# Two attention layers in one kernel: layer 1's projections for the coming units in quarters, and the last unit's sums turned on the tensor engine

## The chip, the cores and the metric

The kernel runs on one core of one Trainium2 chip. A core has a tensor engine (PE in the profile, its weight loads PEld), a vector engine (DVE), a scalar engine (ACT), a gpsimd engine (POOL), and a sync engine (SP) which here only issues DMAs. Each engine works through its own instructions in order; they wait for one another by semaphores. The tensor engine writes to PSUM, eight banks of 128 x 512 fp32 values; everything else lies in SBUF or in HBM. The metric is the time of one execution on the device in microseconds.

## The reference

The input x is 2 x 256 x 64 x 64 in fp32: two images of 256 channels at 4096 places. Two layers follow one another. Layer 0 is a gated attention with four heads of 16 channels; it is not touched here. Layer 1 takes its result:

```python
qkv = jnp.einsum('oc,bchw->bohw', w_qkv, x) + b_qkv[None, :, None, None]
qkv = qkv.reshape(b, HEADS, 3 * head_dim, h * w)
q, k, v = jnp.split(qkv, 3, axis=2)
scale = 1.0 / jnp.sqrt(jnp.asarray(head_dim, x.dtype))
attn = jax.nn.softmax(jnp.einsum('bhdn,bhdm->bhnm', q, k) * scale, axis=-1)
out = jnp.einsum('bhnm,bhdm->bhnd', attn, v).reshape(b, c, h, w)
return jnp.einsum('oc,bchw->bohw', w_out, out) + b_out[None, :, None, None] + x
```

It has four heads of 64 channels, so each query is compared with 4096 keys. Everything is fp32.

## The kernel before

**Units and steps.** Layer 1's attention is cut into 32 units, numbered 0 to 31 here: an image b, a pair g of heads and a block j of 512 queries, j running fastest. The 4096 keys of a unit are 32 chunks of 128, and a step takes two of them, so a unit has 16 steps; US = 16 is that number. The loop at line 1206 goes over all steps t of all units. "Step r of a unit" means its r-th of these 16, from 0 to 15. A unit's scores are weighed and gathered LAG = 11 steps later, so each step holds the scores of one unit and the weighing of chunks 11 steps older. The 16 chunks of a half unit share one shift (their running maximum); a unit has NG = 2 such halves.

**A step.** `score` (line 848) makes the scores of each chunk: two matmuls, one for each head, into a pair of PSUM banks. `keep` takes their running maximum on the vector engine (line 876) and copies them to SBUF on the scalar engine (877), which frees the PSUM pair. `shift` (929) subtracts the shift of an older chunk on the vector engine, `weigh` (941) takes the exponential on the scalar engine and adds it to a sum on gpsimd (953), and `gather` (963) multiplies by the values. On the tensor engine a step is: both chunks' scores, then what hangs in the place "early", then the gather, then what hangs in "late". On the vector engine it is: first maximum, first shift, "early end", second maximum, "late end", second shift. On the scalar engine: exponential of the step before, first copy, first exponential, "early end", second copy.

**What hangs beside it.** `at(t, place, step)` hangs a function on a place of step t; `seq` keeps compute instructions in program order, while DMAs on SP are placed by the framework. All the small PSUM work shares one bank: `misc` (lines 651 and 777; the pool `psm` has one buffer), so each user waits until the one before it has been read. These are, by step r of a unit:

- 0 and 8: the running maximum of a half is transposed (`turn_max`, line 884) and reduced (`fold`, 901), in two parts, early and late; its row goes through HBM and back, and `place_shift` copies it to PSUM on the scalar engine two steps later (921).
- 1: the gathered sums of the unit before are transposed (`turn_sums`) and scaled to rows (`rows`, 1041), early and late.
- 2 and 3: `next_keys` computes the keys for the next eight units' block, one pass of 128 x 512 over 128 of the 256 channels a step, and `store_keys` copies them out on the scalar engine in step 3.
- 5 and 6: `next_values` computes the values, two of four blocks of 128 places a step (four matmuls of 128 x 128), and `store_values` copies them in step 6. Units 0 to 23 do this; keys and values go to HBM and come back when the eight units are done.
- 10 and 11: `next_queries` computes the next unit's queries, one pass a step, kept by `keep_queries` in step 11. Units 0 to 30 do this.
- 12: `total` sums the gpsimd sums over the partitions on the tensor engine (993), and `keep_total` copies the result (1001) and sends it through HBM (1006, 1008) to turn rows into columns; `add_sums` and `factors` make the scale factors of it.

**Output.** In units 18 to 21, image 0's finished attention is projected block by block (`project_out`, 1071, four matmul passes for each image half of 128 channels in two parts o, and `output`, 1079, which adds bias and x on the vector engine and stores after the second part). Even blocks do it in steps 4 and 7, odd ones in 13 and 15, all in the place "early".

**The end.** Image 1's output is projected after the last unit. `last_output` (line 1163) loads what of the attention is finished (1172) and three blocks of x (1176) on SP; `FILL` places the first half of the projection (1182, 1188) between the last steps; the last unit's rows are stored to HBM and read back as `last_att` (1058, 1064), and then the second half is projected (line 1238) and stored.

Of the kernel before, what the change touches and what calls it, by code (L numbers as in the profile page):

```python
# [8 lines left out]
F32 = mybir.dt.float32  # L9
AF = mybir.ActivationFunctionType  # L10
# [4 lines left out]
P = 128  # L15
NB = 512
C = 256
CC = C // P
H = 4
D0 = 16  # L20
D1 = 64
# [5 lines left out]
def conv_attention_kernel(  # L27
# [19 lines left out]
    nc = tc.nc  # L47
    B, _, N = x.shape
    NJ = N // NB
    NM = N // P  # L50
    PB = NB // P
# [3 lines left out]
    small = ctx.enter_context(tc.tile_pool(name="small", bufs=2))  # L55
# [70 lines left out]
    for s in range(3):  # L126
        t = const_prep.tile([P, CC, P], F32, tag=f"wpad{s}", name=f"wpad{s}")
# [11 lines left out]
    ident = const.tile([P, P], F32, tag="ident", name="ident")  # L139
# [72 lines left out]
    def at(t, place, step):  # L212
        extras.setdefault((t, place), []).append(step)
# [19 lines left out]
    with own0:  # L233
# [417 lines left out]
        def misc(name):  # L651
            return small_bank[0](name)
# [6 lines left out]
        def project_in(ps, xt, g, t, c):  # L659
            seq(nc.tensor.matmul(  # L660
                ps, w1[:, c, t, bass.ts(g, P)], xt[:, c, :], start=(c == 0), stop=(c == CC - 1)
            ))
# [21 lines left out]
        def keep_queries(u):  # L684
            b, g, j = u
            q, ps = qs1[u]
            seq(nc.scalar.activation(q, ps, AF.Identity, bias=b1[:, g, 0:1]))
            qs1[u] = q

        def values_in(ps, xt, g, k):  # L690

            for c in range(CC):
                seq(nc.tensor.matmul(
                    ps[:, bass.ts(k, P)], xt[:, c, bass.ts(k, P)], w1[:, c, 2, bass.ts(g, P)],
                    start=(c == 0), stop=(c == CC - 1),
                ))
# [71 lines left out]
    with (  # L768
# [33 lines left out]

        def next_keys(b, g, i, c):
            if c == 0:
                halves_of["k"] = misc(f"k1p_{b}_{g}_{i}")
            project_in(halves_of["k"], loaded["kv", b, g, i], g, 1, c)

        def store_keys(b, g, i):  # L810
            k = l1.tile([P, NB], F32, tag="kv", name=f"k1s_{b}_{g}_{i}")
            seq(nc.scalar.activation(
                k, halves_of.pop("k"), AF.Identity, bias=b1[:, g, 1:2]
            ))
            nc.sync.dma_start(out=kd[b, g, i], in_=k)

        def next_values(b, g, i, k):
            if k == 0:
                halves_of["v"] = misc(f"v1p_{b}_{g}_{i}")
            for n in (k, k + 1):  # L820
                values_in(halves_of["v"], loaded["kv", b, g, i], g, n)

        def store_values(b, g, i):
            loaded.pop(("kv", b, g, i))
            v = l1.tile([P, NB], F32, tag="kv", name=f"v1s_{b}_{g}_{i}")
            seq(nc.scalar.copy(v, halves_of.pop("v")))
            nc.sync.dma_start(out=vd[b, g, i], in_=v)

        def load_keys(b, g, i):
            k = l1o.tile([P, NB], F32, tag=f"k{i}", name=f"k1_{b}_{g}_{i}")  # L830
# [5 lines left out]
            nc.sync.dma_start(out=v.rearrange("p i h d -> p (i h d)"), in_=vd[b, g, i])  # L836
            vs[b, g, i] = v

        def next_queries(u, c):
            b, g, j = u  # L840
            if c == 0:
                q = l1x.tile([P, NB], F32, tag="q", name=f"q1_{b}_{g}_{j}")
                qs1[u] = q, misc(f"q1p_{b}_{g}_{j}")
            project_in(qs1[u][1], loaded["q", u], g, 0, c)
            if c == CC - 1:
                loaded.pop(("q", u))

        def score(t):
# [61 lines left out]
        def lose(u):  # L910

            b, g, j = u
            lost = small.tile([P, 2, PB], F32, tag="lost", name=f"lost_{b}_{g}_{j}")
            seq(nc.gpsimd.tensor_tensor(lost, negs.pop((u, 1)), negs.pop((u, 0)), ALU.subtract))
            losts[u] = lost
# [82 lines left out]
        def keep_total(u):  # L998
            b, g, j = u
            row = l1.tile([P, NB], F32, tag="kv", name=f"srow_{b}_{g}_{j}")  # L1000
            seq(nc.scalar.copy(
                row.rearrange("p (a m i) -> p a i m", m=P, i=2),
                srows[u].rearrange("p (a i m) -> p a i m", m=P, i=2),
            ))
            for m in range(2 * NG):
                nc.sync.dma_start(out=sum1[u][m : m + 1, :], in_=row[32 * m : 32 * m + 1, :])
            s = small.tile([P, NG, 2, PB], F32, tag="sums1", name=f"sums1_{b}_{g}_{j}")
            nc.sync.dma_start(
                out=s.rearrange("p n k (a i) -> p (n k a) i", i=2),
                in_=sum1[u].rearrange("m (a p i) -> p (m a) i", p=P, i=2),  # L1010
            )
            srows[u] = s
            seq(nc.scalar.activation(losts[u], losts[u], AF.Exp, scale=D1**-0.5))

        def turned(a, name):
            ps = misc(name)
            for i in range(PB):
                seq(nc.tensor.transpose(ps[:, bass.ts(i, P)], a[:, bass.ts(i, P)], ident))  # L1018
            return ps.rearrange("p (i k d) -> p k i d", k=2, d=D1)

        def add_sums(u):
            s, lost = srows[u], losts[u]
            seq(nc.gpsimd.tensor_tensor(s[:, 0], s[:, 0], lost, ALU.mult))
            seq(nc.gpsimd.tensor_tensor(s[:, 1], s[:, 1], s[:, 0], ALU.add))
# [52 lines left out]
        def output(b, j, o):  # L1077
            xt = loaded["xo", b, j]
            seq(nc.vector.scalar_tensor_tensor(
                xt[:, o, :], outs.pop((b, j, o)), bo1[:, o : o + 1], xt[:, o, :], ALU.add, ALU.add  # L1080
            ))
            if o == CC - 1:
                nc.sync.dma_start(
                    out=out[b, :, bass.ts(j, NB)].rearrange("(c p) n -> p c n", p=P), in_=xt
                )
# [12 lines left out]
        for n, u in enumerate(units):  # L1098
            b, g, j = u
            t0 = n * US  # L1100
            if n > 0:
                at(t0 - 9, "start", lambda u=u, b=b, j=j: fetch(("q", u), x1[b][j]))
                for c in range(CC):
                    at(t0 - 6 + c, "early", lambda u=u, c=c: next_queries(u, c))
                at(t0 - 5, "early end", lambda u=u: keep_queries(u))
            if n < len(units) - NJ:
                to = (*units[n + NJ][:2], j)
                at(max(t0 - 1, 0), "start", lambda to=to: fetch(("kv", *to), x1[to[0]][to[2]]))
                for c in range(CC):
                    at(t0 + 2 + c, "early", lambda to=to, c=c: next_keys(*to, c))  # L1110
                at(t0 + 3, "early end", lambda to=to: store_keys(*to))
                at(t0 + 5, "early", lambda to=to: next_values(*to, 0))
                at(t0 + 6, "early", lambda to=to: next_values(*to, 2))
                at(t0 + 6, "early end", lambda to=to: store_values(*to))

                t1 = (n // NJ * NJ + NJ - 1) * US
                at(t1 + 2 * j + 2, "start", lambda to=to: load_keys(*to))
                at(t1 + 2 * j + 3 + LAG, "start", lambda to=to: load_values(*to))
            for k in range(NG):
                t1 = t0 + (k + 1) * GS // 2  # L1120
                for i, place in enumerate(("early", "late")):
                    at(t1, place, lambda u=u, k=k, i=i: turn_max(u, k, i))
                    at(t1, f"{place} end", lambda u=u, k=k, i=i: fold(u, k, i))
                at(t1 + 2, "end", lambda u=u, k=k: place_shift(u, k))
            t1 = t0 + US + GS // 2
            at(t1 + 4, "early", lambda u=u: total(u))
            at(t1 + 4, "early end", lambda u=u: keep_total(u))
            at(t1 + 1, "late", lambda u=u: lose(u))
            at(t1 + 5, "late end", lambda u=u: add_sums(u))
            at(t1 + 7, "start", lambda u=u: factors(u))  # L1130
            for place, k in (("early", 1), ("late", 0)):
                at(t1 + 9, place, lambda u=u, k=k: turn_sums(u, k))
                at(t1 + 9, f"{place} end", lambda u=u, k=k: rows(u, k))
            if b < B - 1 and (g, j) == (PR - 1, NJ - 1):
                for i in range(NJ):
                    t1 = t0 + US + (i + 4) * GS // 2
                    at(t1, "start", lambda b=b, i=i: fetch_output(b, i))
                    for o, step in enumerate((t1 + 4 + i % 2, t1 + 7)):
                        at(
                            step, "early",  # L1140
                            lambda b=b, i=i, o=o: project_out(b, i, o, misc(f"o1_{b}_{i}_{o}")),
                        )
                        at(step, "early end", lambda b=b, i=i, o=o: output(b, i, o))

# [146 lines left out]
```

## Time and profile before

| | us |
|---|---|
| median of 3 runs | 4735.43 (4734.52 to 4735.52) |
| the profiled execution | 4733.19, span 4731.4 |
| busy: PE / DVE / ACT / POOL | 4486.2 / 3901.4 / 3428.9 / 2496.6 |
| one ordinary unit of layer 1, from one unit's sums to the next's | 80.4 |
| one without next keys and values (units 24 to 30) | 78.6 |
| those with output projections (18 to 21) | 83.7 to 91.9, as the sums of step 12 cut them |

The span begins with the program's first instruction and ends with its last; the small rest of the execution's time lies around it. Layer 0 takes the first 2080 us and is the same in both kernels. Matmuls are pipelined, so their busy time overstates their work a little, and one fp32 matmul leaves two records. A wait of an engine is put down to what ended it; in a step that is full on all engines, the time is set by the one that never waits, and a wait of that one is what costs. Where a length in us is named without a view, it is the difference of two starts in the timeline.

### The profile page before, as it was taken

How to read it: one execution, taken by the hardware profiler on the slowest of the kernel's cores; microseconds unless marked ns; L12 is line 12 of the kernel's file. 1: busy time of each engine (PE TensorE's matmuls, PEld its weight loads, DVE VectorE, ACT ScalarE, POOL GpSimd, SP SyncE). 2: the span in 40 equal slices, each digit the busy share in tenths (PEclk: the TensorE clock that was granted, in tenths of full speed). 3: DMA queues.
4: the chain of work that ended last, by engine and by line, in shares of the span. 5: the costliest groups of instructions: out<-in, count | busy, mean ns of one | idle time of the engine just before them, and what ended most of it. 6: DMA issues, size and time to landing. Idle time of an engine off the chain costs nothing. (4 is left out here: it accounts for less than half of the span.)

```text
span 4731.4 us, 70140 instructions
## 1 busy us (share of the span) xinstructions
PE 4486.2 (95%) x26998; PEld 1464.4 (31%) x26998; DVE 3901.4 (82%) x4520; ACT 3428.9 (72%) x4508; POOL 2496.6 (53%) x1294
## 2 busy tenths in 40 slices
PE   8999999999999999989999999999999999898997
PEld 3433333333333333332222322222232222222222
DVE  6777777777777777359999999999998899999996
ACT  3366666666666666668888888888887788888884
POOL 5300000000000000029999999999988889999994
PEclk9999999999999999999999999999999999999999
DMA  3100000000000000121111221112222222111113
GB/s 103 34 4 19 19 20 16 15 15 15 15 15 15 15 13 13 57 63 39 34 41 34 66 45 34 41 34 54 59 52 65 65 63 56 37 26 23 26 34 83
DMA packets 200211, 174.67 MB, mean 37 GB/s; under 512 B 122168, under 2 KB 123000, under 8 KB 199748
## 3 DMA queue, kind: packets, MB, share of 16 engines
q1 hardware_dynamic: 198068, 169.60, 14.2%
q8 instruction: 212, 3.47, 0.3%
q14 instruction: 123, 1.01, 0.1%
q10 hardware_dynamic: 1808, 0.59, 0.1%
HBM read 127.66 MB, written 42.48 MB: 36 GB/s over the span
## 5 line engine op out<-in xcount | busy, mean ns | idle before, releaser
L953 POOL TENSOR_TENSOR acc<-acc,raw 128x1024 f32<-128x1024 f32 x883 | 2095.1, 2373 | 106.0 <-ACT raw L941 52.0
L402 DVE TENSOR_REDUCE mx<-a 128x1 f32<-128x512 f32 x2048 | 1314.5, 685 | 451.1 <-PE a L398 449.9
L439 ACT ACTIVATE p<-s 128x512 f32<-128x512 f32 x2048 | 1108.0, 595 | 702.6 <-PE a L398 369.1
L859 PE MATMUL s<-q,k 64*128 64x512 f32 x4096 | 1127.3, 639 | 180.3 <-ACT raw L877 175.5
L929 DVE TENSOR_TENSOR raw<-raw,shift 128x1024 f32<-128x1024 f32 x1024 | 1233.7, 1208 | 10.6 <-ACT shift L921 10.1
L876 DVE TENSOR_TENSOR rmax<-s,rmax 128x1024 f32<-128x1024 f32 x960 | 1167.0, 1216 | 88.7 <-PE s L859 85.6
L436 PE MATMUL s<-q,kT 32*128 32x512 f32 x4096 | 1218.5, 640 | 0.0
L877 ACT COPY raw<-s 128x1024 f32<-128x1024 f32 x1024 | 1035.4, 1011 | 237.9 <-DVE rmax L876 170.4
L941 ACT ACTIVATE raw<-raw 128x1024 f32<-128x1024 f32 x1024 | 1086.1, 1061 | 137.9 <-DVE raw L929 102.1
L398 PE MATMUL a<-kT,q 32*128 32x512 f32 x4096 | 1130.0, 643 | 0.9 <-DVE mx L402 0.8
L963 PE MATMUL av<-raw,v 128*64 128x512 f32 x4096 | 999.1, 606 | 6.3 <-ACT raw L941 6.0
L451 PE MATMUL av<-p,v 128*32 128x256 f32 (+1 forms) x7904 | 650.1, 399 | 0.6 <-ACT avs L465 0.6
L859 PEld LDWEIGHTS s<-q,k 64*128 64x128 f32 x4096 | 317.3, 185 | 921.1 <-ACT raw L877 725.0
L501 POOL TENSOR_TENSOR f<-f,dyn 128x16 f32<-128x16 f32 x15 | 3.3, 221 | 1028.1 <-DVE f L500 1028.1
L436 PEld LDWEIGHTS s<-q,kT 32*128 32x128 f32 x4096 | 397.4, 183 | 426.2 <-issue 392.8
L963 PEld LDWEIGHTS av<-raw,v 128*64 128x64 f32 x4096 | 243.8, 136 | 618.4 <-issue 465.2
L451 PEld LDWEIGHTS av<-p,v 128*32 128x32 f32 x7904 | 157.6, 108 | 751.5 <-issue 737.3
L552 POOL TENSOR_SCALAR res<-res 128x1024 f32<-128x1024 f32 x16 | 16.7, 1045 | 661.9 <-ACT res L551 661.9
L398 PEld LDWEIGHTS a<-kT,q 32*128 32x128 f32 x4096 | 304.8, 183 | 31.6 <-DVE mx L402 18.5
L951 POOL TENSOR_TENSOR acc<-raw,raw 128x1024 f32<-128x1024 f32 x64 | 152.5, 2382 | 157.1 <-ACT raw L941 157.1
L901 DVE TENSOR_REDUCE negs<-rt 128x4 f32<-128x512 f32 x128 | 88.1, 689 | 51.0 <-PE rt L884 50.9
L306 DVE RECIPROCAL std<-std 128x128 f32<-128x128 f32 x64 | 56.1, 919 | 37.4 <-ACT std L301 37.4
(319 smaller groups left out, 1721.9 us busy)
## 6 DMA issues: line engine op xcount, KB each, us to landing
row<-neg SPq DMA_DIRECT2D x128, 256.0 KB
x<-in_x_dram SPq DMA_DIRECT2D x16, 512.0 KB
res<-in_x_dram SPq DMA_DIRECT2D x16, 512.0 KB
x<-res SPq DMA_DIRECT2D x16, 512.0 KB
att<-rows SPq DMA_DIRECT2D x63, 128.0 KB
kd<-k1s SPq DMA_DIRECT2D x24, 256.0 KB
vd<-v1s SPq DMA_DIRECT2D x24, 256.0 KB
k<-kd SPq DMA_DIRECT2D x24, 256.0 KB
```

The lines of the kernel that those rows point to most:

```text
L398: seq(nc.tensor.matmul(ps, qs0[u][r, bass.ts(i, P)], kTs[b][r, bass.ts(m, NB)], start=True, stop=True,))
L402: seq(nc.vector.tensor_reduce(mxs[u][:, i * H + h, m : m + 1], ps, AX.X, ALU.max))
L436: seq(nc.tensor.matmul(ps, kTs[b][r, bass.ts(m, P)], qs0[u][r, :], start=True, stop=True))
L439: seq(nc.scalar.activation(pt[:, k, :], ps, AF.Exp, scale=D0**-0.5))
L451: seq(nc.tensor.matmul(avs[u][32 * h : 32 * h + 32, cols], vs0[b][:, m, 32 * h : 32 * h + 32], pts[t, h // 2][:, h % 2, cols], start=(m == ...
L859: seq(nc.tensor.matmul(ps[:, k, :], ks[b, g, m // PB][r, bass.ts(m % PB, P)], qs1[u][r, :], start=True, stop=True,))
L876: seq(nc.vector.tensor_tensor(rmax[u, n], ps, before, ALU.max))
L877: seq(nc.scalar.copy(raw, ps))
L929: seq(nc.vector.tensor_tensor(raws[t], raws[t], shifts[u, t % NM // GS], ALU.add))
L941: seq(nc.scalar.activation(p, p, AF.Exp, scale=D1**-0.5))
L953: seq(nc.gpsimd.tensor_tensor(accs[u, n], accs[u, n], p, ALU.add))
L963: seq(nc.tensor.matmul(avs1[u, n][k * D1 : (k + 1) * D1, :], v[:, m % PB, k, :], raws[t][:, k, :], start=(m % GS == 0), stop=(m % GS == GS ...
```

## The change

**Quarters.** `quarter` computes half of the channels' pass for half of the columns: one matmul of 128 x 256, where `project_in` had one of 128 x 512. Keys take one quarter in each of steps 2, 3, 4 and 5 and are stored in step 5. Values take one block of 128 places in each of steps 6, 7, 9 and 10; each pair has its own use of the misc bank and its own half copy on the scalar engine, in steps 7 and 10. Queries take two quarters in step 11 and one each in 13 and 14, with half copies in 11 and 14; the misc bank is thus free for the sums in step 12.

**Output projections.** Even blocks go to steps 5 and 7, odd ones to 12 and 15; all but the last of these four lie in the place "late", behind the gather.

**The last unit's sums.** They are copied as they lie, transposed on the tensor engine (`turn_total`, four transposes into the misc bank) and copied by the vector engine into the form in which the others come from HBM. The five DMAs of the last unit's sums are gone.

```diff
-        def next_keys(b, g, i, c):
-            if c == 0:
+        def quarter(ps, xt, g, t, q):
+
+            c, cols = q % 2, bass.ts(q // 2, NB // 2)
+            seq(nc.tensor.matmul(
+                ps[:, cols], w1[:, c, t, bass.ts(g, P)], xt[:, c, cols],
+                start=(c == 0), stop=(c == CC - 1),
+            ))
+
+        def next_keys(b, g, i, q):
+            if q == 0:
                 halves_of["k"] = misc(f"k1p_{b}_{g}_{i}")
-            project_in(halves_of["k"], loaded["kv", b, g, i], g, 1, c)
+            quarter(halves_of["k"], loaded["kv", b, g, i], g, 1, q)
...
-        def next_values(b, g, i, k):
-            if k == 0:
-                halves_of["v"] = misc(f"v1p_{b}_{g}_{i}")
-            for n in (k, k + 1):
-                values_in(halves_of["v"], loaded["kv", b, g, i], g, n)
+        def next_values(b, g, i, q):
+            if q % 2 == 0:
+                halves_of["vp"] = misc(f"v1p_{b}_{g}_{i}_{q}")
+            values_in(halves_of["vp"], loaded["kv", b, g, i], g, q)
...
+        def store_values(b, g, i, half):
+            if half == 0:
+                halves_of["v"] = l1.tile([P, NB], F32, tag="kv", name=f"v1s_{b}_{g}_{i}")
+            v, cols = halves_of["v"], bass.ts(half, NB // 2)
+            seq(nc.scalar.copy(v[:, cols], halves_of.pop("vp")[:, cols]))
+            if half == 1:
+                loaded.pop(("kv", b, g, i))
+                nc.sync.dma_start(out=vd[b, g, i], in_=v)
...
+            if q % 2 == 0:
+                halves_of["q"] = misc(f"q1p_{b}_{g}_{j}_{q}")
+            quarter(halves_of["q"], loaded["q", u], g, 0, q)
+
+        def keep_next_queries(u, half):
+            cols = bass.ts(half, NB // 2)
+            seq(nc.scalar.activation(
+                qs1[u][:, cols], halves_of.pop("q")[:, cols], AF.Identity,
+                bias=b1[:, u[1], 0:1],
+            ))
+            if half == 1:
                 loaded.pop(("q", u))
...
             row = l1.tile([P, NB], F32, tag="kv", name=f"srow_{b}_{g}_{j}")
+            if u == units[-1]:
+                seq(nc.scalar.copy(row, srows[u]))
+                seq(nc.scalar.activation(losts[u], losts[u], AF.Exp, scale=D1**-0.5))
+                srows[u] = row
+                return
...
+        def turn_total(u):
+
+            ps = misc("sumt")
+            for i in range(PB):
+                seq(nc.tensor.transpose(ps[:, bass.ts(i, P)], srows[u][:, bass.ts(i, P)], ident))
+            s = small.tile([P, NG, 2, PB], F32, tag="sums1", name="sums1_last")
+            seq(nc.vector.tensor_copy(
+                s.rearrange("p n k i -> p i (n k)"),
+                ps.rearrange("p (i m e) -> p i m e", i=PB, e=32)[:, :, :, 0],
+            ))
+            srows[u] = s
...
-                for c in range(CC):
-                    at(t0 - 6 + c, "early", lambda u=u, c=c: next_queries(u, c))
-                at(t0 - 5, "early end", lambda u=u: keep_queries(u))
+                for q in range(4):
+                    at(t0 - (5, 5, 3, 2)[q], "early", lambda u=u, q=q: next_queries(u, q))
+                at(t0 - 5, "early end", lambda u=u: keep_next_queries(u, 0))
+                at(t0 - 2, "early end", lambda u=u: keep_next_queries(u, 1))
...
-                for c in range(CC):
-                    at(t0 + 2 + c, "early", lambda to=to, c=c: next_keys(*to, c))
-                at(t0 + 3, "early end", lambda to=to: store_keys(*to))
-                at(t0 + 5, "early", lambda to=to: next_values(*to, 0))
-                at(t0 + 6, "early", lambda to=to: next_values(*to, 2))
-                at(t0 + 6, "early end", lambda to=to: store_values(*to))
+                for q in range(4):
+                    at(t0 + 2 + q, "early", lambda to=to, q=q: next_keys(*to, q))
+                    at(t0 + (6, 7, 9, 10)[q], "early", lambda to=to, q=q: next_values(*to, q))
+                at(t0 + 5, "early end", lambda to=to: store_keys(*to))
+                for i, step in enumerate((t0 + 7, t0 + 10)):
+                    at(step, "early end", lambda to=to, i=i: store_values(*to, i))
...
+            if u == units[-1]:
+                at(t1 + 5, "early", lambda u=u: turn_total(u))
...
-                    for o, step in enumerate((t1 + 4 + i % 2, t1 + 7)):
+                    for o in range(CC):
+                        step = t1 + ((5, 7), (4, 7))[i % 2][o]
+                        place = "early" if i % 2 and o else "late"
                         at(
-                            step, "early",
+                            step, place,
                             lambda b=b, i=i, o=o: project_out(b, i, o, misc(f"o1_{b}_{i}_{o}")),
                         )
-                        at(step, "early end", lambda b=b, i=i, o=o: output(b, i, o))
+                        at(step, f"{place} end", lambda b=b, i=i, o=o: output(b, i, o))
```

More of the change, by code (lines that the diff above doesn't have):

```diff
@@ L815, in store_keys @@
             nc.sync.dma_start(out=kd[b, g, i], in_=k)
-        def next_values(b, g, i, k):
-            if k == 0:
-                halves_of["v"] = misc(f"v1p_{b}_{g}_{i}")
-            for n in (k, k + 1):
-                values_in(halves_of["v"], loaded["kv", b, g, i], g, n)
[L823 to L827, printed above, removed]
+        def next_values(b, g, i, q):
[10 more added lines that the diff above has]
+                nc.sync.dma_start(out=vd[b, g, i], in_=v)
         def load_keys(b, g, i):
@@ L837, in load_values, with next_queries @@
             vs[b, g, i] = v
-        def next_queries(u, c):
+        def next_queries(u, q):
             b, g, j = u
[L841 to L845, printed above, removed]
+            if q == 0:
+                qt = l1x.tile([P, NB], F32, tag="q", name=f"q1_{b}_{g}_{j}")
+                qs1[u] = qt
+            if q % 2 == 0:
[8 more added lines that the diff above has]
+            if half == 1:
                 loaded.pop(("q", u))
```

## The prediction

> **What bounds the kernel now.** I read the waits of the vector engine in layer 1 first, then the busy sums of single units, then the timeline of three kinds of step, and last the chain that ended last. In what follows "step r" is step r of a unit's 16; s0 and s1 are the two score pairs of a step on the tensor engine (L859), rmax0 and rmax1 their maxima on the vector engine (L876), copy0 and copy1 their copies on the scalar engine (L877).
>
> The waits of the vector engine from 2080 us on (total, times, longest):
>
> ```profile
> DVE rmax L876 <- PE s L859: 83.2, 166, 1.3
> DVE negs L901 <- PE rt L884: 50.9, 95, 2.8
> ```
>
> Three units by window, an ordinary one, one with output projections, one without next keys (window, length, then busy time of PE, PEld, DVE, ACT, POOL):
>
> ```profile
> 2428.80:2509.20 80.40, 75.03 (x314) 23.35 (x312) 75.83 (x71) 69.72 (x75) 74.27 (x36) 1.00 0.16 37
> 3557.50:3646.70 89.20, 82.89 (x330) 25.97 (x328) 78.87 (x75) 69.79 (x75) 74.18 (x36) 1.00 0.25 69
> 4299.00:4377.70 78.70, 71.29 (x294) 20.63 (x292) 75.63 (x71) 68.98 (x73) 74.31 (x37) 1.00 0.14 24
> ```
>
> The vector engine is busy 75.8 of 80.4 us and the tensor engine 75.0: the vector engine bounds a unit and loses 4.6 us in it, to late scores and to the turned maxima. A unit without keys and values is only 1.7 us shorter, though 3.7 us of tensor time are gone: most of that work is hidden already. So the pool that a better spread can win is small: 1.7 us in 23 units, and 0.7 in 30 for the queries (from one copy0 to the next, step 11 takes 4.87 us with them and 4.18 in the last unit, which computes none).
>
> A step that carries half the values, one with an output projection and a plain one, from the timelines of the tensor and of the vector engine (start, us):
>
> ```profile
> 3033.76 1.16 PE L693 MATMUL v1p<-w,xb_('kv', 1, 0, 4)_24784 128*128 128x128 f32 x8
> 3034.85 1.94 PE L963 MATMUL av<-raw,v 128*64 128x512 f32 x8
> 3036.72 1.13 PE L859 MATMUL s<-q,k 64*128 64x512 f32 x4
> ...
> 3617.00 1.98 PE L1071 MATMUL o<-ao_('ao', 0, 2)_28123,wo 128*128 128x512 f32 x4
> ...
> 4590.32 1.13 PE L859 MATMUL s<-q,k 64*128 64x512 f32 x4
> 4591.92 1.13 PE L859 MATMUL s<-q,k 64*128 64x512 f32 x4 [0.47 <-ACT raw L877]
> 4592.98 1.94 PE L963 MATMUL av<-raw,v 128*64 128x512 f32 x8
> 4594.85 1.13 PE L859 MATMUL s<-q,k 64*128 64x512 f32 x4
> ```
>
> ```profile
> 3037.89 1.23 DVE L876 TENSOR_TENSOR rmax<-s,rmax 128x1024 f32<-128x1024 f32 x1 [0.69 <-PE s L859]
> ...
> 3619.03 0.75 DVE L1079 SCALAR_TENSOR_TENSOR xo_('xo', 0, 2)_28121<-o,bo,xo_('xo', 0, 2)_28121 128x512 f32<-128x512 f32 x1 [0.74 <-PE o L1071]
> ...
> 4591.82 1.22 DVE L876 TENSOR_TENSOR rmax<-s,rmax 128x1024 f32<-128x1024 f32 x1
> ```
>
> They give the rules of the sum. A score pair can be read 1.17 us after its start (3036.72 to 3037.89). s0 follows s1 by 2.93 us plus the step's extra work X (4591.92 to 4594.85, where X is 0), or by 2.82 plus X where s1 came straight after s0, 0.97 behind it. rmax0 repeats every 4.52 us, rmax1 is 2.26 behind it, copy1 1.30 behind rmax1, and s1 of the next step 1.07 behind copy1. So s0 has 0.33 us to spare in a plain step (4590.32 + 1.17 against 4591.82); what exceeds it becomes idle time of the vector engine, and the 0.47 us for which s1 waits anyway keeps the lateness from piling up. An extra ahead of copy1 on the scalar engine has 0.23 to spare (the next instruction can follow an exponential by 0.96, copy1 starts 1.19 behind it).
>
> The end, from the chain of waits (start, us):
>
> ```profile
> 4686.52 9.00 DMA sum_(1, 1, 7)_19383<-srow
> ...
> 4702.19 2.58 DMA att<-rows
> ...
> 4704.91 5.50 DMA last_att<-att
> ```
>
> The last unit's sums cross HBM behind 3.25 MB of loads on SP's queue (L1172, L1176), and all that leads to the last projection (4710.51) waits for them.
>
> **What the Trainium skill says.** "PSUM — Partial Sum Buffer", PSUM bank collisions: two engines on one bank are kept apart by a dependency, reads included. The trace agrees: copy0 starts 0.08 us after rmax0 ends. The one "misc" bank thus serializes its users. "DMA: Bandwidth & Descriptors", queues, rings and completion order: SP's copies stand in one ring on each of the 16 DMA engines, taken in order; here four copies of 2 KB took 9.00 us. "TensorE: Matmul & The Clock Gate", what's actually happening: an idle window of about 3.4 us halves the clock. Here eight records of L1182 took 5.57 us at 4700.37, after 13.5 us of idling, and 3.70 at 4680.09.
>
> **Ordinary units (1 to 23).** The matmul work stays. A pass of 128x512 costs 1.06 us (3063.88 to 3064.94), half the values 1.09 (3033.76 to 3034.85), a block of 128 columns of them thus 0.545. Time goes with columns from the one to the other, so I take 0.53 for a quarter of 256. New X: 0.53 in steps 2 to 5, 0.545 in 6, 7, 9 and 10, 1.06 in 11 (two quarters), 0.53 in 13 and 14. I carry the rules on from rmax0 of step 2 of a unit without keys (4254.57).
> Steps 2 to 4: s0 has 0.90 us to spare in step 3, 0.21 in 4, 0.07 in 5; rmax0 of step 5 gets 0.47 late (0.61 before). In step 5 the key store (0.57 in a row) slips copy1 by 0.34, and s1 of step 6 with it; with the first block of values rmax0 of step 7 is 1.04 late. Step 7's block adds 0 to 0.1; its half store (0.3) all but fits. At step 8 the lateness is 1.1, where the traced units with and without keys differ by 1.74 (29.02 and 27.28 us from rmax0 of step 2): gain 0.63. The same rules give the starts of the unit before, as traced, within 0.1 us.
> Step 9 has 1.13 us of waiting on the tensor engine: free. Step 10 loses a query pass and gets a block: 0.23 late. In 11 a half keep (0.33) replaces a keep (0.57), but the scalar engine is back to back from 10 to 12: 0.31 is won by step 13, and 0.10 given back in 14. Gain 0.21.
> Sum: 0.84 x 23 = 19.3 us. Units 24 to 30 have queries alone: 0.28 x 7 = 2.0. On SP the loads of x now stand behind the moved stores, but each is fetched about a unit ahead of its use: nothing. Unit 0, whose steps have no gather: nothing.
>
> **Output projections (units 18 to 21).** Three of four move from the early place to the late one. Before, the four cost 1.84, 1.51, 1.29 and 1.52 us (their steps less those of ordinary units). Late, the 1.92 us of matmuls stand behind the gather; the vector engine has done rmax1 by then and idles until they end, and the last shift and rmax0 of the next step are queued behind L1079. In step 5 they also wait until the key store frees the bank. By the rules the pair of steps 5 and 7 costs 5.5 against 3.35 (3.4 in step 5, part of it in place of lateness that is there anyway), step 12, behind the sums' matmuls, 2.66 against 1.29; step 15 stays. Loss 3.6 x 4 = 14.4 us. The store of an even block goes out 1.1 us nearer to the maxima of step 8; their row is issued by 3631.5 and used at 3637.19 without a wait: nothing.
>
> **The end.** Four transposes (0.6), a small vector copy (0.2, as the reciprocal of 8 columns), then the old steps: rows of half 1 start at 4686.3 instead of 4698.71. Late next is L1188 of the sixth block, ahead of half 0's rows on the vector engine: its load ends at about 4690.3 (3.25 MB move from 4680.0 to 4694.5). The att store goes out at 4693.2, not 4702.2, lands behind the last load, is read back from 4696.6 for 5.5 us, and the projection starts at 4702.1, not 4710.5: 8.4 us. The half clock may take 0 to 2 of it: 7.5. Bounds 4 and 10.
>
> **Sum.** 19.3 + 2.0 - 14.4 + 7.5 = 14.4 us off the profiled execution's 4733.2 (span 4731.4): 4718.8. The runs' median is 2.2 above it: 4721.
>
> **Rivals.** (a) The quarters hide entirely: 1.7 x 23 + 0.7 x 30 = 60 us, 7.5 at the end, less 14: 4682. For it: 0.47 us of tensor waiting in a plain step is nearly a quarter. Against: s0 has only 0.33, and the scalar engine its backlog. (b) Gain and loss cancel: projections cost 5 us more a unit, the ordinary gain is 0.5: 13 - 20 + 7 = 0, 4735. (c) Slower: a group of matmuls has a cost of its own beyond its columns. A unit gets 11 groups of such work instead of 6. The value records show none, but no quarter of 256 columns is in the trace; bounds 0 and 0.4 us. From 0.2 us on it decides: at 0.3 the 5 more cost 1.5, the gain of 0.84 turns into a loss of 0.66 x 23 = 15, and 15 + 14 - 7 = 22 us: 4757. (d) The turn at the end gains 3 us, as the store queues behind loads: 4725, inside the forecast.
>
> **How the numbers follow.** Forecast (with d) 0.60, (a) or half of it 0.10, (b) 0.19, (c) 0.11. An error of 0.3 us in a unit's gain is 8 us, of 1 us in the projections 4, at the end 3: its own range is 4709 to 4732. For 8 in 10 with the others: 4701 to 4744. The measurement tells about 0.2%, 9.5 us: faster 0.66, same 0.22, slower 0.12.
>
> **What would show it.** Units of 79.5 us instead of 80.4, of 78.4 instead of 78.7 where only queries are left, 90 to 95 in units 18 to 21, where L1079 waits longer for PE; waits of rmax for PE in small pieces over steps 5 to 7; no sums in the last chain, and the last projection 23 us after the last gather instead of 31. Wrong it would be if a quarter costs over 0.2 us in a plain step, if late projections cost nothing, or if a row of maxima comes late in step 10.

## The result and the profile after

| | before | after |
|---|---|---|
| median of 20 runs each, us | 4737.51 (4734.52 to 4740.97) | 4730.76 (4725.74 to 4734.27) |
| the profiled execution (span), us | 4733.19 (4731.4) | 4731.40 (4729.6) |

The change takes 6.75 us off; the ratio is 0.9985, with a 95% interval of 0.9978 to 0.9992. The two profiled executions lie only 1.8 us apart, because that of before is 4.3 us below its kernel's median and that of after 0.6 above. So the parts below are read in units and steps, which repeat within 0.05 us but for single late rows of maxima (rows that come back from HBM after their step wants them), and summed against the medians.

The waits of the vector engine in layer 1 of after (total, times, longest), and ahead of them the one of before that the prediction does not show:

```profile
DVE raw L929 <- ACT shift L921: 10.1, 6, 3.1
DVE rmax L895 <- PE s L878: 59.2, 130, 1.6
DVE negs L920 <- PE rt L903: 49.1, 91, 1.5
DVE raw L948 <- ACT shift L940: 17.6, 15, 3.7
```

The scores are late by 59 us in all instead of 83, in 130 places instead of 166. That is what quarters were to do. But 24 us less waiting did not make 24 us: added up over all of image 0's blocks, the waits for projections (L1079 before, L1115 after) rose from 15.6 to 33.2 us, and those for late shifts from 10.1 to 17.6. Of these 7.5 us only 2.5 lie in units 19 to 22; the others are single late rows. The profiled execution of before had few of those, which fits its lying so far below its median.

Three units by window, ordinary (12), with projections (20) and without next keys (27), here from copy0 to copy0, first before, then after; columns as in the prediction, which shows other units, cut at the sums:

```profile
3007.60:3087.90 80.30, 74.93 (x314) 23.35 (x312) 75.74 (x71) 69.73 (x74) 74.20 (x37) 1.00 0.17 37
3665.40:3757.30 91.90, 85.99 (x330) 26.88 (x328) 78.93 (x75) 69.72 (x74) 74.18 (x36) 0.96 0.25 66
4243.90:4322.50 78.60, 71.19 (x294) 20.64 (x292) 75.52 (x71) 68.88 (x73) 74.25 (x37) 1.00 0.12 24
```

```profile
2999.20:3079.00 79.80, 75.68 (x322) 24.76 (x320) 75.97 (x71) 69.50 (x76) 74.23 (x37) 1.00 0.17 37
3661.60:3757.30 95.70, 86.14 (x338) 28.53 (x336) 78.62 (x75) 69.73 (x76) 74.10 (x36) 0.96 0.24 63
4248.00:4326.50 78.50, 71.64 (x298) 21.24 (x296) 75.66 (x71) 68.75 (x73) 74.17 (x37) 1.00 0.14 25
```

The ordinary unit is shorter by 0.5 us and unit 27 by 0.1, at nearly the same busy time of the vector engine. Unit 20 has grown from 91.9 to 95.7.

Step by step, from the start of copy0 to that of the next step (us; units 18 to 22 stand beside unit 12, which has no projection):

| step of unit 12 | 2 | 3 | 4 | 5 | 6 | 7 | 11 | 13 | 14 | whole unit |
|---|---|---|---|---|---|---|---|---|---|---|
| before | 5.34 | 4.75 | 4.23 | 5.31 | 4.87 | 4.52 | 4.87 | 4.52 | 4.59 | 80.35 |
| after | 5.33 | 4.18 | 4.78 | 4.53 | 5.19 | 4.53 | 4.53 | 4.56 | 4.82 | 79.83 |

| what a projection adds to its step, unit 18 less unit 12 | first | second | first, odd block | second, odd block | given back or added next to them | sum |
|---|---|---|---|---|---|---|
| before (steps 4, 7, 13, 15) | 1.85 | 1.51 | 1.29 | 1.52 | 0 | 6.2 |
| after (5, 7, 12, 15) | 3.35 | 3.04 | 2.64 | 1.39 | -0.67 in 6, -0.36 in 8 | 9.4 |

Step 5 of unit 20 in after, first the tensor engine's timeline, then the vector engine's (start, us, and in brackets the idle time ahead with its releaser):

```profile
3693.70 1.94 PE L982 MATMUL av<-raw,v 128*64 128x512 f32 x8
3696.40 1.98 PE L1107 MATMUL o<-ao_('ao', 0, 4)_28774,wo 128*128 128x512 f32 x4 [0.76 <-ACT k1s L820]
```

```profile
3694.60 1.22 DVE L895 TENSOR_TENSOR rmax<-s,rmax 128x1024 f32<-128x1024 f32 x1
3698.42 0.75 DVE L1115 SCALAR_TENSOR_TENSOR xo_('xo', 0, 4)_28772<-o,bo,xo_('xo', 0, 4)_28772 128x512 f32<-128x512 f32 x1 [2.61 <-PE o L1107]
```

The projection waits 0.76 us for the bank behind the key store, although the gather ahead of it is done, and the vector engine, which has nothing else in its order, idles 2.61 us until it ends.

The chain that ended last, first two pieces of before, then after:

```profile
4678.88 0.44 PE late_sums L973 x2
...
4710.51 15.68 PE o L1182 x32
```

```profile
4683.40 0.44 PE late_sums L992 x2
...
4684.78 12.03 DMA x_last<-x
...
4697.59 0.74 DVE x_last L1229
4698.34 0.61 DVE rows L1077
4698.99 0.04 issue
4699.04 0.70 DVE rows L1088
4699.76 2.56 DMA att<-rows
...
4702.47 5.69 DMA last_att<-att
4708.16 0.09 issue
4708.25 16.36 PE o L1223 x32
```

The last unit's sums cross HBM no more. What is late next is the x block of L1229, as predicted. From the end of the sums' matmuls to the projection it is 24.4 us (4708.25 - 4683.84) instead of 31.2 (4710.51 minus 4679.32, the end of L973), and the projection itself takes 16.36 instead of 15.68: 6.1 us in all.

### The profile page after: what moved, and what is told of

It is laid out like the page before. It is cut to its first block, busy times and chain, and to the rows that moved or that the text cites. A ratio compares the mean times of both kernels' runs of the same rounds, so it can differ in the third digit from the quotient of the medians.

```text
span 4729.6 us, 70682 instructions
## 1 busy us (share of the span) xinstructions
PE 4509.2 (95%) x27222; PEld 1503.3 (32%) x27222; DVE 3905.8 (83%) x4521; ACT 3423.9 (72%) x4563; POOL 2496.6 (53%) x1294
## 3 DMA queue, kind: packets, MB, share of 16 engines
q1 hardware_dynamic: 197020, 169.58, 14.4%
## 5 line engine op out<-in xcount | busy, mean ns | idle before, releaser
L948 DVE TENSOR_TENSOR raw<-raw,shift 128x1024 f32<-128x1024 f32 x1024 | 1236.1, 1211 | 19.0 <-ACT shift L940 17.6
```

The source lines that it names most:

```text
L948: seq(nc.vector.tensor_tensor(raws[t], raws[t], shifts[u, t % NM // GS], ALU.add))
```

## The experiments

E1 to E3 take the change apart; E4 moves the work that had become dear; E5 to E8 test reasons one by one; E9 and E10 measure the disputed price. Ratios are against before, with 95% intervals. E1 to E4, E5 to E8, and E9 with E10 ran in three groups on three chips, each with runs of before beside it: 4738.31, 4736.87 and 4738.61 us. A difference between kernels of two groups is uncertain by these 2 us as well.

**E1: the turned sums alone.** Before, with `turn_total`, its call and the branch of `keep_total` that copies the last sums as they lie; nothing else.

> The kernel before with the last unit's sums turned on the tensor engine, and nothing else of the change. Theory (the three parts add up; the end is worth what the trace of after shows, 31.2 us from the end of the last gather to the last projection before and 24.4 after, less 0.7 for the half clock): 6 us less than before, about 4731.5. Rival (the end gives only 3 us alone, and the whole change's 6.75 us stem from its loops): about 4734.5.

Measured 4731.08, before beside it 4738.31: ratio 0.9985 (0.9978 to 0.9991), 7.2 us less. The end carries its part alone, and it is as large as what the whole change brings. So the loops' gains and losses must nearly cancel, within the 3 us of the interval.

**E2 and E3: both kernels without the projections.**

```diff
-            if b < B - 1 and (g, j) == (PR - 1, NJ - 1):
-                for i in range(NJ):
...
```

> The kernel before without the output projections of image 0 and their loads and stores: it leaves that output out. Units 18 to 21 took 86.5, 89.2, 91.9 and 88.2 us against 80.4. Theory (all of this excess is the projections'): 34 us less than before, about 4703. Rival (part of the excess is traffic or late rows of maxima that stay): 25 us less or fewer.

> The changed kernel without the output projections of image 0: it leaves that output out. Theory (late projections cost 14 us more than early ones; quarters gain 4 in unit 0 and some 0.5 a unit after it, 14 in all; the end 6): 49 us less than after, about 4682, and 20 us less than the kernel before without them. Rival (the projections cost the same in both places and the quarters gain next to nothing): 34 us less than after, 4697, and some 7 us less than the kernel before without them.

Measured 4700.56, ratio 0.9918 (0.9905 to 0.9932), and 4679.38, ratio 0.9875 (0.9860 to 0.9891). The projections thus cost 37.8 us early (4738.31 - 4700.56) and 51.4 late (4730.76 - 4679.38): the move loses 13.6. Without them the change gains 21.2, of which 7.2 is the end if it is worth the same here: the quarters are worth 14.0. That 14.0 - 13.6 + 7.2 comes near 6.75 proves nothing, since all three are differences of the same medians and have to add up to the change.

A test is the sum of the steps, which does not use the medians. Ordinary units give 23 x 0.52 us, units with queries alone 7 x 0.06 and unit 0 about 0.5 (see below): 12.9 for the quarters. Projections lose 4 x 3.2 = 12.8, and the end gains 6.1. 12.9 - 12.8 + 6.1 = 6.2, against 6.75. Late rows, which differ from one execution to the next, are left out of it.

**E4: the projections moved to units 24 to 31.** These compute no keys and values, so the misc bank and the tensor engine have room where the others have none.

```diff
...
-                    t1 = t0 + US + (i + 4) * GS // 2
-                    at(t1, "start", lambda b=b, i=i: fetch_output(b, i))
...
+                    t1 = END - (NJ - i) * US
+                    at(t1 - 2, "start", lambda b=b, i=i: fetch_output(b, i))
+                    for o, steps in enumerate(((2, 3, 4, 5), (6, 7, 9, 10))):
+                        for q, step in enumerate(steps):
+                            at(t1 + step, "early",
+                               lambda b=b, i=i, o=o, q=q: project_out(b, i, o, q))
...
-            at(END - 12 + 2 * i, "start", lambda i=i: fetch_last(i))
+            at(END - 12 + 2 * i + (i >= 3), "start", lambda i=i: fetch_last(i))
```

> The changed kernel with image 0's output projections in units 24 to 31, which compute no keys and values: one block a unit, in quarters of 256 columns in the steps and places of the keys and values (2 to 5, 6 and 7, 9 and 10, early), bias and sum on the vector engine in steps 5, 7 and 10. Theory (a quarter hides where the step has room, and the vector engine's 0.75 + 2 x 0.42 us are all that a unit pays, with 0.3 us of lateness): 49 us go in units 18 to 21, 8 x 1.9 = 15 come, about 4697. Rival (the loads of output blocks and the stores delay the rows of maxima or the last loads of x, or a projection costs 3.6 us wherever it is): no gain on after, 4720 to 4735.

Measured 4700.77, ratio 0.9921 (0.9907 to 0.9934): 37.5 us faster than before and 30 faster than after. The edit changes three things at once, the units, the cut of each projection into quarters and the place, and no run parts them. The window of a unit that now holds a block, and of an ordinary one:

```profile
4204.10:4285.00 80.90, 75.87 (x314) 23.81 (x312) 77.37 (x74) 68.85 (x73) 74.23 (x37) 1.00 0.19 43
2991.00:3070.90 79.90, 75.71 (x321) 24.80 (x321) 76.01 (x71) 69.57 (x76) 74.25 (x37) 1.00 0.18 37
```

A block costs 2.4 us (unit 27: 80.93 from copy0 to copy0, against 78.55 in after). In after, two blocks cost 9.6 to 15.9 us in each of units 18 to 21 (89.39 to 95.77 against 79.83). Of the 2.4, 1.7 is vector work (77.37 against 75.66), which nothing hides. The late rows of maxima of units 19 to 22 are gone too: in layer 1 up to 4720 us the waits for shifts are

```profile
DVE raw L948 <- ACT shift L940: 7.6, 17, 1.2
```

instead of 17.6 us, the longest 1.2 instead of 3.7.

**E5: the output loads two steps later.** `at(t1, "start", ...)` of `fetch_output` becomes `at(t1 + 2, "start", ...)`.

> The changed kernel with the loads of a block of output (x and attention, 512 KB each) two steps later, in steps 2 and 10 instead of 0 and 8, so behind the rows of maxima on SP's queue. Theory (at step 0 the load of x waits for the store of the block before, issued 4.5 us earlier, and keeps SP from the row of maxima behind it; its shift comes late in step 2, which takes 7.3 to 9.0 us in units 19 to 22 against 5.3 elsewhere): steps 2 to 4 of these units fall to 5.3, 4.2 and 4.8, and 12 us go, about 4719. Rival (the late row is due to other traffic, or the loads now come late for the projections of steps 4 and 5): no more than 3 us, 4728 or over.

Measured 4729.88, ratio 0.9986 (0.9979 to 0.9992): no gain on after. The timelines of SP's queue tell why, after first, then E5:

```profile
3658.32 0.38 SPq L1119 DMA_DIRECT2D out_dram<-xo_('xo', 0, 3)_28520  x1
3662.87 0.36 SPq L656 DMA_DIRECT2D xo_('xo', 0, 4)_28772<-x  x1
3663.28 0.46 SPq L923 DMA_DIRECT2D neg<-negs  x1
```

```profile
3659.05 0.38 SPq L1119 DMA_DIRECT2D out_dram<-xo_('xo', 0, 3)_28588  x1
3663.68 0.36 SPq L656 DMA_DIRECT2D xo_('xo', 0, 4)_28852<-x  x1
3664.09 0.46 SPq L923 DMA_DIRECT2D neg<-negs  x1
```

The order is the same: store, load of x, and then the row of maxima (L923). The framework places DMAs on SP by itself, and the later call did not move the load behind the row. So neither theory was tested. That the row suffers from the block's load and store ahead of it remains an argument; E2 and E3, without them, show only that the wait needs these projections or their traffic (7.7 us in E3).

**E6 and E7: keys and values alone, queries alone.** The quarters of each on before without projections.

> The kernel before without image 0's output projections, with the keys and values in the new quarters and the queries as before: it leaves image 0's output out. Against the same without the quarters (4700.6). Theory (the keys and values carry the gain, 0.46 us a unit by the steps of the traces, and 1.4 in unit 0): 12 us less, 4688.5. Rival (the gain is as much the queries'): 7 us less, 4693.5.

> The kernel before without image 0's output projections, with the queries in the new quarters and the keys and values as before: it leaves image 0's output out. Against the same without the quarters (4700.6). Theory (step 11 gains 0.34 us and steps 13 and 14 give 0.26 back): 0.07 us a unit, 2 us less, 4698.5. Rival (as predicted, 0.21 to 0.28 a unit): 7 us less, 4693.5.

E6 took 4762.79 us, ratio 1.0055 (1.0042 to 1.0067), 62 us more than E2, against both expectations. Steps 2 to 9 of its unit 12 are those of after, but step 10 takes 7.86 us and not 5.33. There the last block of values and the old first pass of the queries meet in the misc bank; the tensor engine, then the vector engine:

```profile
3087.03 0.71 PE L693 MATMUL v1p<-w,xb_('kv', 1, 0, 4)_24832 128*128 128x128 f32 x4
3089.61 1.12 PE L660 MATMUL q1p<-b_('q', (0, 1, 5))_25062,w 128*128 128x512 f32 x2 [1.87 <-ACT v1s L834]
3090.67 1.94 PE L973 MATMUL av<-raw,v 128*64 128x512 f32 x8
```

```profile
3093.71 1.23 DVE L886 TENSOR_TENSOR rmax<-s,rmax 128x1024 f32<-128x1024 f32 x1 [3.24 <-PE s L869]
```

The query pass waits 1.87 us for the half copy of the values, the gather waits behind the pass, and the next scores behind the gather. E6 says nothing of the keys' gain, but it shows what the queries' move is for: two users of the one bank in one early place cost 2.5 us in step 10, and 2.7 in the unit (82.49 against 79.83).

E7 took 4696.49, ratio 0.9914 (0.9901 to 0.9928), 4.1 less than E2, between the two expectations; with each set against before in its own group, it is 2.6 less. Step 11 takes 4.53 instead of 4.87, step 14 4.84 instead of 4.59; a unit is 0.05 us shorter (unit 12 80.32 and not 80.36; unit 27 78.56, and 78.61 in before). The steps thus give under 2 us, and the rest is within what the two groups differ by and what single late rows (step 2 of units 3, 16 and 22 in E2) make of a run. With the queries at 2 to 4, the keys and values get 10 to 12 of the 14.0.

**E8: the place late, in the old steps.** Before, with `"late"` for all but the last of the four projections.

> The kernel before with the output projections in its own steps (4 and 7, 13 and 15), but all except the last of these four in the place late, as the change has it. Theory (the place alone makes them dear: the matmuls stand behind the gather and the vector engine waits for their end): 3 us a unit more than early, 12 us in all, about 4750. Rival (late costs no more than early, and it is the new steps 5 and 12, where the key store or the sums stand ahead of it): 0 to 3 us more, 4738 to 4741.

Measured 4741.68, ratio 1.0011 (1.0002 to 1.0019), 4.8 more than before: nearer to the rival. Steps 4, 7 and 13 cost 2.56, 1.89 and 2.0 us instead of 1.85, 1.51 and 1.29, and 0.7 comes back in steps 5, 6 and 8: 7.3 us a unit instead of 6.2. Step 4 of its unit 20:

```profile
3694.14 1.94 PE L963 MATMUL av<-raw,v 128*64 128x512 f32 x8
3696.00 1.98 PE L1071 MATMUL o<-ao_('ao', 0, 4)_28614,wo 128*128 128x512 f32 x4
```

```profile
3698.03 0.75 DVE L1079 SCALAR_TENSOR_TENSOR xo_('xo', 0, 4)_28612<-o,bo,xo_('xo', 0, 4)_28612 128x512 f32<-128x512 f32 x1 [1.14 <-PE o L1071]
```

Here the projection follows the gather at once. This unit is disturbed by a late row, and in step 4 of the others the vector engine idles 1.81 to 2.41 us; but in step 7 it idles 1.14 in all four, against 2.29 in after and 0.74 in before. By the steps, the place alone is 1.1 of the 3.2 us that a unit loses. The rest goes with the new steps, in which more stands ahead of the late projection: in 5 the key store that frees the bank (0.76 us of waiting, shown above), in 7 a block of values (0.64 us of tensor time), in 12 the sums' matmuls (1.00). That these three make up the rest is argued, not shown by a run of its own.

**E9: the price of a group by itself.** E4, with a matmul of 64 columns more in step 15.

```diff
+            ps, q = misc(f"thin_{n}"), qs1[units[n]]
+            seq(nc.tensor.matmul(
+                ps[:, :64], w1[:, 0, 1, bass.ts(g, P)], q[:, :64], start=True, stop=True
+            ))
...
+            at(t0 + 15, "early", lambda n=n, g=g: thin(n, g))
```

> The kernel with image 0's output projections in units 24 to 31, and in step 15 of every unit one matmul more, of 64 columns into the misc bank, which nothing reads. It measures what a group of such work costs by itself. In the trace of after, a group of 256 columns took 0.63 us from its start to the next start and one of 512 took 1.06. Theory (a group costs 0.20 us and 0.43 for 256 columns): 0.31 us from its start to the next start for 64 columns. Rival (as predicted, in proportion to the columns): 0.13 us. Either hides in step 15, which has 0.33 us to spare: 4700 to 4702.

One run, 4698.97 us; step 15 takes 4.30 us as it did, so the matmul is hidden, as both expected. The tensor engine of E9, and a quarter of after:

```profile
3074.41 0.44 PE L815 MATMUL thin<-q,w 128*128 128x64 f32 x2
3074.78 1.94 PE L988 MATMUL av<-raw,v 128*64 128x512 f32 x8
```

```profile
3015.61 0.70 PE L808 MATMUL k1p<-xb_('kv', 1, 0, 4)_24880,w 128*128 128x256 f32 x2
3016.24 1.94 PE L982 MATMUL av<-raw,v 128*64 128x512 f32 x8
```

From start to next start, 64 columns take 0.37 us, a quarter 0.63 and a pass 1.06: a group has a price of its own. At 64 columns it is above what either expected (0.31 and 0.13); its two weight loads of 0.188 us each would fit that, which is only argued.

**E10: an uneven cut.** E4, with the keys cut at column 320.

```diff
-            c, cols = q % 2, bass.ts(q // 2, NB // 2)
+            c, cols = q % 2, (slice(0, cut), slice(cut, NB))[q // 2]
...
-            quarter(halves_of["k"], loaded["kv", b, g, i], g, 1, q)
+            quarter(halves_of["k"], loaded["kv", b, g, i], g, 1, q, 320)
```

> The kernel with image 0's output projections in units 24 to 31, its next keys cut at column 320 instead of 256, so that the quarters of steps 2 and 3 have 320 columns and those of steps 4 and 5 have 192. Theory (the lateness of rmax0 of step 5 is the group of step 4 less what it has to spare; a group costs 0.20 + 0.43 for 256 columns, so it shrinks by 0.11 us while step 3, with room, takes as much more): step 4 takes 4.67 instead of 4.77 us and a unit 79.72 instead of 79.83; 23 units give 2.5 us, about 4698.3. Rival (step 3 has no room left, so that the work only turns late one step earlier): step 3 longer by what step 4 is shorter, 4700.8.

The tensor engine in steps 3 and 4 of unit 12 of E10:

```profile
3014.71 0.81 PE L808 MATMUL k1p<-xb_('kv', 1, 0, 4)_24880,w 128*128 128x320 f32 x2
3015.44 1.94 PE L982 MATMUL av<-raw,v 128*64 128x512 f32 x8
3017.31 2.38 PE L878 MATMUL s<-q,k 64*128 64x512 f32 x8
3019.62 0.59 PE L808 MATMUL k1p<-xb_('kv', 1, 0, 4)_24880,w 128*128 128x192 f32 x2
3020.14 1.94 PE L982 MATMUL av<-raw,v 128*64 128x512 f32 x8
```

The groups take 0.73 and 0.52 us. Step 4 takes 4.65, step 3 4.18 as it did, and the unit 79.72, all as the theory said. The time is 4699.14, ratio 0.9919 (0.9906 to 0.9933); 1.6 us less than E4, which the runs don't tell from nothing, though the trace does. With E4, from which the runs don't part it, it is the fastest kernel here that does the whole work.

## Why the prediction was right, and where it was too high

The forecast was a gain of 14.4 us, and 6.75 came, less than half of it. The time lies in the forecast's own range, 4709 to 4732, but near its slow end, and that range was wide for a change of this size. Sign and mechanism were right: quarters take lateness out of the steps, late projections cost, and the end gains.

- **The rules** (1.17 us from scores to maxima, 2.93 + X, room of 0.33) hold: with the right X they gave what step 4 and the whole unit of E10 take to 0.02 us.
- **Ordinary units: here the size was off.** 0.84 a unit was predicted, 0.52 came (80.35 - 79.83): 0.48 instead of 0.63 up to step 8, 0.06 instead of 0.21 in steps 11 to 14. For the queries alone 0.06 came instead of 0.28. The failing term is "I take 0.53 for a quarter of 256". It scaled whole passes in proportion to columns; a quarter took 0.63, a block of values 0.64 instead of 0.545. The four sizes from 192 to 512 columns (0.52, 0.63, 0.73, 1.06) lie on 0.20 us for a group and 0.43 for 256 columns. "Time goes with columns from the one to the other" compared two groups of 512 columns each, 1.06 and 1.09, and each holds one such price, so these could not show it. But before had two sizes of one kind, in the same place between scores and gather, one pass and the two passes of a projection:

```profile
3063.88 1.12 PE L660 MATMUL q1p<-b_('q', (0, 1, 5))_25021,w 128*128 128x512 f32 x2
3064.94 1.94 PE L963 MATMUL av<-raw,v 128*64 128x512 f32 x8
...
3617.00 1.98 PE L1071 MATMUL o<-ao_('ao', 0, 2)_28123,wo 128*128 128x512 f32 x4
3618.92 1.94 PE L963 MATMUL av<-raw,v 128*64 128x512 f32 x8
```

From start to next start one pass takes 1.06 us and two take 1.92: 0.86 for the second, and so 0.20 that is paid once. The prediction used both numbers, and had 0.43 + 0.20 for a quarter within its reach. The surplus of 0.1 falls where a step has no room: step 4 (4.78, where the prediction's lateness of 0.47 would give 4.67), which E10 confirms, and steps 6 and 14, which is only argued (14 gave back 0.23 instead of 0.10). Quarters brought 14.0 us by the medians and 12.9 by the steps, where 21.3 was predicted: this is nearly the whole shortfall.

- **Unit 0 was costed at nothing and gained a little.** Its steps 3 to 7 have no gather, and quarters hide in them wholly: 13.3 us in all instead of 14.3, in every trace. Steps 11 to 14 give some 0.45 back, which leaves 0.5. The length of the whole unit does not show this better, since its step 2 varies by 1 us between traces: it is 61.2 to 62.8 us with the quarters of after, and 62.3 to 65.15 in the loop of before, where the longest has a step 8 of 7.94 instead of 5.26. A gain that the forecast did not count is luck, here a small piece of it.
- **Output projections were right.** Predicted 5.5 for steps 5 and 7 with what is given back, measured 5.36; 2.66 and 2.64 for step 12; 14.4 us in all and 13.6. (Its own parts make 3.5 us a unit, not 3.6: 5.5 - 3.35 and 2.66 - 1.29.) The steps give 12.8 of the 13.6. The reason was right too: it named the gather, the key store and the sums that stand ahead, but gave no shares; by E8 the place behind the gather is a third of it.
- **"The row is used without a wait: nothing"** does not hold in step 10 of unit 20, where the vector engine waits 0.46 us for the shift and the step takes 6.10 us instead of 5.34; in units 18, 19 and 21 no such wait stands there. A row late in step 10 was one of the prediction's own signs of being wrong; it came once, and cost under 1 us. More was overlooked in step 2 of units 19 to 22, where the row of half 1 is late in both kernels: 9.1 us in sum before and 10.5 after, over 5.34 each. As both have it, it spoils the difference by 1.4 us only.
- **The end was right.** 7.5 was predicted; 7.2 came by the medians of E1 and 6.1 by the chains, and the step was the one named: the x block is late next. It landed 13.0 us after the sums' matmuls, where the forecast put 11.0 (4690.3 - 4679.3), so the projection starts 6.8 us earlier and not 8.4, and it takes 0.7 more by itself.
- **The rivals.** (a), 60 us, is refuted by the 14.0 of E1 to E3. (c) was right that a group has a cost of its own: 0.20 us, at the point from which the prediction let it decide. With 5 more groups a unit its sum would turn the gain of 0.84 into a loss of 0.16, and 0.52 of gain came: it counts every group as lost, while many fall where a step has room (in E10 step 3 stayed at 4.18 us with 0.10 more in it). (b) had the ordinary gain (0.5, measured 0.52) but projections too dear (5 us a unit more, measured 3.2); that the loops nearly cancel is what it said, and 6.75 lies halfway between its 0 and the forecast's 14.4. (d), 3 us at the end, lies outside E1's interval (4.3 to 10.4 us).

## What to carry to other kernels

Before work is cut into smaller groups, take the start-to-start time of two sizes of the same matmul and fit a price per group and per column; scaling one size understates the price of a cut. The trace at hand may already hold the two sizes, as it did here. Where one PSUM bank serves many users, an extra user is dear where another's copy stands ahead of it (2.5 us in E6), so move it to steps in which the bank is free: here that, with the cut into quarters, was worth 30 us, twice what the cutting of the projections for keys, values and queries gave. And where a framework places the DMAs, look at the queue in the trace before crediting an edit with a new order.

## What the hardware showed that was not expected

A group of fp32 matmuls between groups of other operands cost 0.20 us beyond its columns, once for the group and not for each matmul in it (1.06 and 1.92 us for one and two passes). The Trainium skill ("TensorE: Matmul & The Clock Gate", "Single matmul latency") gives a bf16 matmul by itself, at full clock, a constant of about 166 ns plus its columns; no run here shows that it is the same constant. And at 64 columns a group did not fall below 0.36 us.
